# A gated graph network on one core: the order inside the third tick, the place of a relu, and the engine of a subtraction

## The chip, the cores and the metric

The kernel runs on one core of a Trainium2 chip. The metric is the device time of one execution, in microseconds (us). Engines are named as in the profile: PE is TensorE (matrix products; PEld is its loading of weights), DVE is VectorE, ACT is ScalarE, POOL is GpSimd, SP is SyncE, which here only issues transfers (DMAs). Each engine works through its own list of instructions in order, and waits at an instruction until what it needs from others is there.

## The reference, cut to what matters

```python
# x: (64, 256, 256) float32, adj: (64, 256, 256) int32
def gru_cell(inp, h):                      # w_ih, w_hh: (768, 256)
    i_r, i_z, i_n = split(inp @ w_ih.T + b_ih)
    h_r, h_z, h_n = split(h @ w_hh.T + b_hh)
    r = sigmoid(i_r + h_r)
    z = sigmoid(i_z + h_z)
    n = tanh(i_n + r * h_n)
    return (1.0 - z) * n + z * h

h = maximum(layernorm(x), 0.0)             # layer A: gated graph network
for i in range(3):
    m = h @ weight[i]
    aggr = einsum('bst,bsd->btd', adj != 0, m)
    h = gru_cell(aggr, h)
x = x + h
h = maximum(layernorm(x), 0.0)             # layer B: graph attention, 4 heads
v = h @ W.T + b
logits = leaky_relu(l_src + l_dst, 0.2)    # l_src, l_dst: v times a, per head
probs = softmax(where(adj == 1, logits, -9e15))
x = x + einsum('bijh,bjhc->bihc', probs, v)
```

In the last line of the cell, (1 - z) n + z h is n + z (h - n). It is this `h - n` that the change touches.

## The kernel before, in words

**Tiling.** The 64 batch elements are taken in 32 pairs. State, sums and gates lie transposed: 128 partitions, two halves (`c` = 0, 1) of the 256 features, and 2 x 256 nodes of the pair along the free dimension; element `i` = 0 or 1 of the pair is one half of it. A square product of 256 features for one element (`block`, L313) is four fp32 matmuls of 128x128 on 128x256, and each such matmul is two records in the profile, so a block shows as x8.

**Steps and ticks.** One layer of the gated network for one pair is a `Step` of six ticks, `tick_0` to `tick_5` (L459 to L550). A plan (`at`, and `ready`, `step`, `rest` in `plan_pair`) puts every piece of work at a tick number. Pairs start 18 ticks apart (`APART`), and the three steps of a pair start at ticks 0, 12 and 24 of it, so that in any 18 ticks there are three steps one after the other: layer 0 of pair p, layer 2 of pair p - 1, layer 1 of pair p. The profile shows these as steps of 22.4, 25.5 and 28.5 us, and their sum, 76.4 us, as a period. Attention work of earlier pairs is spread over the same ticks.

**What sets the order.** Within a tick the phases are STEP, READY, REST, and in a phase the later pair comes first (L1033: `for tick in sorted(plan)`). The scheduler is off (`manual_schedule`): each engine's list is in the order in which the plan calls the functions. A fractional tick is a tick of its own between two others, so what stands there comes after all of the tick before.

**Products and sums.** The gates of both elements are built from fewer products with sums and differences of weights and states. The names that matter here, with buffer numbers and trailing digits left out in the profile (`p5` shows as `p`, `m5` as `m`, `T1` to `T4` as `T`):

- `state_sums` (L431): T1 = h1 - h0, T3n and T2n, by VectorE, three ticks ahead of their step; `last_state_sum` (L440): T4n.
- `tick_0`: the first part of the state's n gate into bank `qa`, the aggregation `pa` (L470), copied by ScalarE to `aggr` (L474).
- `tick_1`: the part NS2 into `qb` (L482), then VectorE writes the second half of `qb` from its first (L483); block `pc` with `w_h`; ScalarE copies `pc` to `pd` (L489); T3 and T2 by VectorE (L491, L492).
- `tick_2`: parts NS3 and NS4 into the two halves of `qb` (L496, L497; the matmul's own line is L448), VectorE's `hn` from the first half (L498), ScalarE's `hn` from the second (`state_n`, L451), block `p5` from T1, copied by ScalarE to `m5` (L503), T4 by VectorE (L504).
- `tick_3`: block S2 into `pd` from T2, VectorE's `pe` = `pd` + `m5` (L509), block RA into `pc`, tanh of the r gate (L455).
- `tick_4`: a last part into `qb` from T4n, `first_n(0)` (L525), block RZ into `pd` (L518, which writes the bank that L509 reads), Z by VectorE (L519), block S4 into `pe`.
- `tick_5`: `first_n(1)`, the n gate's blocks `pn0` and `pn1`, block ZA into `pd` from T4; `new_n` (L532): tanh by ScalarE (L536), then h - n into `R` by POOL (L540).
- `update(i)` (L552), in the READY phase of the tick after the step: R = (Z + 1) R (L557), h = R / 2 + n (L558), both by VectorE. These are thus in VectorE's list behind `tick_0` and ahead of `tick_1` of the following step.

After `update`, `back` (L788) turns h back by PE (`pback`, L807), ScalarE rounds it to `hNhi` (L797), VectorE writes the remainder `hNlo` (L798); after the last layer VectorE adds the turned h to x instead (L813).

**The relu.** From the third pair on, the normalised rows `xn_a` (L353) are made at tick -10 of their pair; at tick -10 too, in the READY phase, ScalarE takes their relu in place (L771); at tick -9 VectorE splits them in 16 bit words (`halve`, L387), which two DMAs of SP write out (L389) and read back transposed (L393). Tick -10 of a pair falls in the third tick of a layer-2 step. In that tick's READY phase ScalarE also has an attention operation of an earlier pair, `zz<-link` (L921), and in its REST phase the `hNhi` of the second element; the values of the attention, `val` (L868), their `score` (L876) and the transpose of it by PE (`pscore`, L886) belong to the same step.

The banks of PSUM: 5 for the gates (`ps_g`), taken in turn, 3 for the rest (`ps_m`).

Of the kernel before, what the change touches and what calls it, by code (L numbers as in the profile page):

```python
# [14 lines left out]
AF = mybir.ActivationFunctionType  # L15
# [3 lines left out]
P = 128  # L19
# [8 lines left out]
def gated_gnn_then_gat_kernel(  # L28
# [39 lines left out]
    nc = tc.nc  # L68
    B, N, D = x.shape
# [4 lines left out]
    KD = D // P  # L74
# [3 lines left out]
    T = PB * N  # L78
# [121 lines left out]
    w_a = [const.tile([P, KD, 6 * D], F32, name=f"w_a_{l}") for l in range(L)]  # L200
    RH, RZ = range(2)
    N00, N01, N11, NS1, NS2, NS3, NS4 = range(7)
    RA, ZA, NA, S1, S2, S4 = range(6)
# [99 lines left out]
    def flat(y):  # L303
        return y.rearrange("q r d -> q (r d)")
# [4 lines left out]
    def block(pt, w, j, src, start=False):  # L309

        for c in range(KD):
            for k in range(KD):
                nc.tensor.matmul(  # L313
                    pt[:, ts(c, N)], w[:, k, j * D + c * P : j * D + (c + 1) * P], src[:, k, :],
                    start=start and c == 0 and k == 0, stop=(c == KD - 1 and k == KD - 1),
                    skip_group_check=True,
                )
# [9 lines left out]
    def at(tick, phase, p, fn):  # L327
        plan.setdefault(tick, ([], [], []))[phase].append((-p, fn))

    def plan_norm(src, name, p, ticks, relu=False):  # L330


        v = {}

        def stats(r0):
            def fn():
                if not v:
                    v["st"] = small.tile([P, R, 6], F32, tag="st", name=f"st_{name}")
                    v["mv"] = small.tile([P, R, 2], F32, tag="mv", name=f"mv_{name}")
                for r in (r0, r0 + 1):  # L340
                    nc.vector.bn_stats(v["st"][:, r, :], src()[:, r, :])
                    nc.vector.bn_aggr(v["mv"][:, r, :], v["st"][:, r, :])
            return fn

        def deviation():
            rstd = v["rstd"] = small.tile([P, R], F32, tag="rstd", name=f"rstd_{name}")
            nc.vector.tensor_scalar_add(rstd, v["mv"][:, :, 1], EPS)
            nc.gpsimd.tensor_tensor(rstd, rstd, mhalf, ALU.pow)

        def result():  # L350
            xn = v["xn"] = buf("xn", [P, R, D], f"xn_{name}")
            for r in range(R):
                nc.vector.tensor_scalar(  # L353
                    xn[:, r, :], src()[:, r, :], v["mv"][:, r, 0:1], 0.0 if relu else v["rstd"][:, r : r + 1],
                    op0=ALU.subtract, op1=ALU.max if relu else ALU.mult,
                )

        for t, fn in zip(ticks, (stats(0), stats(2), deviation, result)):
            at(t, READY, p, fn)
        return v  # L360

    def plan_relu_T(v, tag, name, p, ticks):

        w = {}

        def fn(k):
            def go():
                if not w:
                    w["hT"] = buf(tag, [P, KD, T], f"hT_{name}")
                pt = bank(f"pt_{name}_{k}")  # L370
                for r in range(R):
                    nc.tensor.transpose(pt[:, ts(r, P)], v["xn"][:, r, ts(k, P)], ident)
                nc.scalar.activation(w["hT"][:, k, :], pt, AF.Relu)
            return go

        for k, t in enumerate(ticks):
            at(t, REST, p, fn(k))
        return w

    def plan_turn(src, tag, name, p, ticks):  # L380


        w = {}

        def halve():
            words = buf("words", [P, R, 2, D], f"words_{name}", U16)
            nc.vector.tensor_copy(words, src().bitcast(U16).rearrange("q r (d w) -> q r w d", w=2))  # L387
            w["rows"] = dram.tile([R, P, 2 * D], U16, tag="words", name=f"words_dram_{name}")
            nc.sync.dma_start(w["rows"].rearrange("r q e -> q r e"), words.rearrange("q r w d -> q r (w d)"))  # L389

        def turn():
            w["turned"] = buf("turned", [P, 2, KD * T], f"turned_{name}", U16)
            nc.sync.dma_start_transpose(  # L393
                w["turned"].rearrange("q w (k n) -> q (w k) n", k=KD), w["rows"].rearrange("r q e -> (r q) e")
            )

        def join():
            w["hT"] = buf(tag, [P, KD, T], f"hT_{name}")
            nc.vector.tensor_copy(
                flat(w["hT"]).bitcast(U16).rearrange("q (n w) -> q n w", w=2), w["turned"].rearrange("q w n -> q n w")  # L400
            )

        at(ticks[0], READY, p, halve)
        at(ticks[1], REST, p, turn)
        at(ticks[2], READY, p, join)
        return w

    def by_c(y):
        return y.rearrange("q (c n) -> q c n", c=KD)

    def of(y, i):
        return y[:, :, ts(i, N)]

    class Step:
# [77 lines left out]
            nc.vector.tensor_add(self.own("T2", [P, KD, N]), T3, h0)  # L492

        def tick_2(self):
            q_b = self.qb
            self.part(q_b[:, :N], NS3, self.T3n)  # L496
            self.part(q_b[:, N:], NS4, of(self.hT(), 1)[:, 1, :])  # L497
            nc.vector.scalar_tensor_tensor(  # L498
                of(self.hn, 1)[:, 1, :], q_b[:, :N], bhn[:, 1:2], self.m5n, op0=ALU.add, op1=ALU.add
            )  # L500
            self.state_n(0, 1, q_b[:, N:])
            block(self.p5, w_a[self.l], S1, self.T1, start=True)
            nc.scalar.copy(self.own("m5", [P, T]), self.p5)  # L503
            nc.vector.tensor_sub(self.own("T4", [P, KD, N]), self.T2, of(self.aggr, 0))  # L504

        def tick_3(self):
            R_ = self.own("R", [P, KD, T])
# [24 lines left out]
        def new_n(self, i):  # L532
            n__ = of(self.hn, i)
            p_n = by_c(getattr(self, f"pn{i}"))
            for c in range(KD):
                nc.scalar.activation(  # L536
                    n__[:, c, :], p_n[:, c, :], AF.Tanh, bias=bi[:, 2 * KD + c : 2 * KD + c + 1]
                )
            if not (self.end and i == 1):
                nc.gpsimd.tensor_sub(of(self.R, i), of(self.hT(), i), n__)  # L540

        def tick_5(self):
# [9 lines left out]
        def update(self, i):  # L552

            d_ = of(self.R, i)
            if self.end and i == 1:
                nc.vector.tensor_sub(d_, of(self.hT(), i), of(self.hn, i))
            nc.vector.scalar_tensor_tensor(d_, of(self.Z, i), 1.0, d_, op0=ALU.add, op1=ALU.mult)  # L557
            nc.vector.scalar_tensor_tensor(of(self.hT(), i), d_, 0.5, of(self.hn, i), op0=ALU.mult, op1=ALU.add)  # L558
# [181 lines left out]
    def plan_pair(p):  # L740
# [5 lines left out]
        def ready(t, fn):  # L746
            at(t0 + t, READY, p, fn)
# [20 lines left out]
        xn_a = plan_norm(lambda: v["x"], f"a{p}", p, [t0 + t for t in norm_ticks])  # L768
        ready(-1 if p else -2.5, to_edge)
        if dma_a:  # L770
            ready(-10, lambda: nc.scalar.activation(flat(xn_a["xn"]), flat(xn_a["xn"]), AF.Relu))  # L771
            h = plan_turn(lambda: xn_a["xn"], "hT_a", f"a{p}", p, [t0 - 9, t0 - 8, t0 - 3])
        else:
            h = plan_relu_T(xn_a, "hT_a", f"a{p}", p, [t0 - 4, t0 - 3])
# [238 lines left out]
    for p in range(NPAIR):  # L1013
        plan_pair(p)
# [52 lines left out]
```

## Time and profile before

| | |
|---|---|
| time, median of 3 executions | 2521.81 us (2521.77 to 2523.39) |
| the profiled execution's own time | 2522.01 us |
| its span, first to last instruction | 2520.2 us |
| PE busy | 2468.9 us, 98% |
| PEld busy | 2189.5 us, 87% |
| DVE busy | 1947.3 us, 77% |
| ACT busy | 1433.9 us, 57% |
| POOL busy | 630.3 us, 25% |
| mean granted TensorE clock | 0.997 of full speed |

Busy time is that of the profiled execution, as a share of its span. A row of a timeline gives the start and the duration in us, the engine, the source line, the operation, the tile written and the tiles read, the shape, and in brackets the idle time of the engine before it and the instruction that ended that idle time. A row of the list of waits gives the waiting instruction, what it waited for, the time in sum, how often, and the longest. Matmuls are pipelined, and the start of one to the start of the next says more than the duration.

### The profile page before, as it was taken

What the parts mean: (1) busy time and instruction counts of PE and PEld (TensorE: products, weight loads), DVE (VectorE), ACT (ScalarE), POOL (GpSimd) and SP (SyncE); (2) the same over time, 40 slices, a digit from 0 to 9 for tenths busy, and PEclk for the clock granted to TensorE, in tenths of its full rate; (3) what the DMA queues carried; (4) which work ended last, traced back from release to release, by engine and by line L of the source; (5) the groups of instructions that cost most, each with busy time, mean ns of one, the idle gap of its engine ahead of it and who ended that gap; (6) DMA issues with size and microseconds to landing.
All of it is one profiled execution on the core that took longest, in us unless ns stands there. A gap on an engine that the chain in (4) does not pass through costs nothing.

```text
span 2520.2 us, 37693 instructions
## 1 busy us (share of the span) xinstructions
PE 2468.9 (98%) x13446; PEld 2189.5 (87%) x13446; DVE 1947.3 (77%) x4576; ACT 1433.9 (57%) x3007; POOL 630.3 (25%) x514
## 2 busy tenths in 40 slices
PE   8999999999999999999999999999999999999998
PEld 6888888888888888888888888888888888888887
DVE  5678877788777788777878777887777887778767
ACT  3445556555555555556555555555565555665664
POOL 0112232222222232222232322222222222222222
PEclk9999999999999999999999999999999999999999
DMA  3025656555656455656556565556565556564455
GB/s 95 17 59 126 152 117 143 128 124 127 155 114 150 119 124 137 135 125 145 116 128 149 122 139 131 121 126 159 109 151 120 126 133 135 126 148 118 107 115 109
DMA packets 322091, 313.73 MB, mean 124 GB/s; under 512 B 166560, under 2 KB 282224, under 8 KB 321904
## 3 DMA queue, kind: packets, MB, share of 16 engines
q1 hardware_dynamic: 286608, 181.29, 27.1%
q0 software_dynamic: 33728, 130.03, 26.9%
q8 instruction: 106, 1.74, 0.3%
q14 instruction: 81, 0.66, 0.1%
q10 hardware_dynamic: 1568, 0.01, 0.0%
HBM read 215.62 MB, written 56.60 MB: 108 GB/s over the span
## 4 chain that ended last, share of the span: by engine, by line
PE 68%; DVE 23%; ACT 6%; issue 2%; DMA 1%; POOL 0%; DVEq 0%; SPq 0%; ACTq 0%; POOLq 0%
PE pd L313 16%; PE pn L313 9%; PE pc L313 9%; PE po L572 7%; PE pe L313 6%; PE qb L448 5%; PE pa L470 5%; PE p L313 4%; PE qa L448 3%; DVE any L948 3%; DVE hT_a L558 2%; DVE val L868 2%; DVE edge L763 2%; DVE hNlo L798 2%; PE pback L807 2%
## 5 line engine op out<-in xcount | busy, mean ns | idle before, releaser
L540 POOL TENSOR_TENSOR R<-hT_a,hn 128x512 f32<-128x512 f32 x191 | 278.2, 1457 | 1250.2 <-ACT hn L536 1175.5
L313 PE MATMUL pn<-aggr,w_a 128*128 128x256 f32 x1536 | 365.1, 380 | 1.8 <-DVE pn L525 1.8
L313 PE MATMUL pd<-T,w_a 128*128 128x256 f32 x1536 | 366.3, 381 | 0.0
L313 PEld LDWEIGHTS pn<-aggr,w_a 128*128 128x128 f32 x1536 | 286.9, 190 | 43.2 <-DVE pn L525 3.2
L313 PEld LDWEIGHTS pd<-T,w_a 128*128 128x128 f32 x1536 | 288.1, 191 | 37.6
L557 DVE SCALAR_TENSOR_TENSOR R<-Z,R 128x512 f32<-128x512 f32 x192 | 134.3, 700 | 215.9 <-POOL R L540 207.5
L572 PEld LDWEIGHTS po<-val,zz 128*128 128x128 f32 x2048 | 244.9, 192 | 4.5
L948 DVE CUSTOM_DVE_ANT_0 any<-drow,noedge 128x256 f32<-128x256 f32 x496 | 238.0, 480 | 9.7 <-DMA drow<-score_dram 1.0
L536 ACT ACTIVATE hn<-pn,bi 128x256 f32<-128x256 f32 x384 | 160.3, 470 | 146.0 <-PE pn L313 145.8
L572 PE MATMUL po<-val,zz 128*128 128x65 f32 x2048 | 242.1, 272 | 0.0
L588 POOL TENSOR_TENSOR x<-x,o 128x256 f32<-128x256 f32 x124 | 136.9, 1105 | 393.3 <-DVE o L583 372.1
L968 ACT ACTIVATE zz<-zz,val 128x256 f32<-128x256 f32 x496 | 224.2, 506 | 0.0
L455 ACT ACTIVATE R<-pc,brz 128x256 f32<-128x256 f32 x192 | 80.5, 470 | 241.6 <-PE pc L313 241.6
L798 DVE TENSOR_TENSOR hNlo<-pback,hNhi 128x512 fp32r<-128x512 f32 x128 | 88.2, 689 | 150.4 <-ACT hNhi L797 150.4
L455 ACT ACTIVATE R<-pe,brz 128x256 f32<-128x256 f32 x192 | 80.5, 470 | 216.2 <-PE pe L313 216.2
L525 DVE SCALAR_TENSOR_TENSOR pn<-R,hn 128x512 f32<-128x512 f32 x192 | 148.6, 774 | 49.3 <-ACT R L455 32.0
L313 PE MATMUL pd<-T,w_h 128*128 128x256 f32 x768 | 183.6, 382 | 0.2 <-DVE pe L509 0.2
L313 PE MATMUL p<-T,w_a 128*128 128x256 f32 x768 | 181.4, 379 | 0.0
L313 PE MATMUL pc<-hT_a,w_h 128*128 128x256 f32 x768 | 181.4, 379 | 0.0
L313 PE MATMUL pc<-aggr,w_a 128*128 128x256 f32 x768 | 181.4, 379 | 0.0
L313 PE MATMUL pe<-aggr,w_a 128*128 128x256 f32 x768 | 181.4, 379 | 0.0
L313 PEld LDWEIGHTS pd<-T,w_h 128*128 128x128 f32 x768 | 143.5, 190 | 24.7 <-DVE pe L509 6.4
(183 smaller groups left out, 5254.8 us busy)
## 6 DMA issues: line engine op xcount, KB each, us to landing
zz<-score_dram POOLq DMA_DIRECT2D x62, 1024.0 KB, 11.8
zz<-topT_dram POOLq DMA_DIRECT2D x62, 1024.0 KB, 8.8
adj<-in_adj_dram SPq DMA_DIRECT2D x64, 512.0 KB
drow<-score_dram SPq DMA_DIRECT2D x62, 512.0 KB
x<-in_x_dram SPq DMA_DIRECT2D x32, 512.0 KB
out_dram<-x SPq DMA_DIRECT2D x31, 512.0 KB
words_dram_a<-words_a SPq DMA_DIRECT2D x30, 512.0 KB
words_dram_b<-words_b SPq DMA_DIRECT2D x29, 512.0 KB
```

Source lines behind the costliest of these rows:

```text
L313: nc.tensor.matmul(pt[:, ts(c, N)], w[:, k, j * D + c * P : j * D + (c + 1) * P], src[:, k, :], start=start and c == 0 and k == 0, stop=(c ...
L448: nc.tensor.matmul(pt, w_n[:, j, :], src, start=start, stop=True, skip_group_check=True)
L455: nc.scalar.activation(of(dst, i)[:, c, :], src[:, c, :], AF.Tanh, bias=brz[:, g0 + c : g0 + c + 1], scale=0.5)
L525: nc.vector.scalar_tensor_tensor(by_c(self.bank(f"pn{i}")), of(self.R, i), 1.0, of(self.hn, i), op0=ALU.add, op1=ALU.mult)
L536: nc.scalar.activation(n__[:, c, :], p_n[:, c, :], AF.Tanh, bias=bi[:, 2 * KD + c : 2 * KD + c + 1])
L540: nc.gpsimd.tensor_sub(of(self.R, i), of(self.hT(), i), n__)
L557: nc.vector.scalar_tensor_tensor(d_, of(self.Z, i), 1.0, d_, op0=ALU.add, op1=ALU.mult)
L572: nc.tensor.matmul(po[:, ts(h_, VC)], zz[:, j, h_, ts(s, P)], v["val"][:, i * KN + j, ts(h_, VC)], start=(j == 0), stop=(j == KN - 1),)
L588: add(v["x"][:, r, :], v["x"][:, r, :], o)
L798: nc.vector.tensor_sub(lo, pt, hi)
L948: nc.vector.tensor_tensor_reduce(any_, drow[r // KN][:, h, :], v["noedge"][:, r, :], 1.0, -3.0e38, ALU.add, ALU.max, accum_out=v["top"][:, ...
L968: nc.scalar.activation(zz[:, h, :], zz[:, h, :], AF.Prelu, alpha=ALPHA, bias=v["val"][:, r, S0 + H + h : S0 + H + h + 1],)
```

## The change

Three edits. In `tick_2` the block `p5` and the copy of it to `m5` come first, ahead of the two `qb` parts, and T4 comes ahead of VectorE's `hn`. The subtraction h - n of the second element leaves `new_n` (POOL) and is made in `update(1)` by VectorE, which before was so only in the very last step. The relu of `xn_a` is put at tick -9.5 instead of -10. What is computed stays the same. No function is new, and nothing else moves.

```diff
         def tick_2(self):
             q_b = self.qb
+            block(self.p5, w_a[self.l], S1, self.T1, start=True)
+            nc.scalar.copy(self.own("m5", [P, T]), self.p5)
             self.part(q_b[:, :N], NS3, self.T3n)
             self.part(q_b[:, N:], NS4, of(self.hT(), 1)[:, 1, :])
+            nc.vector.tensor_sub(self.own("T4", [P, KD, N]), self.T2, of(self.aggr, 0))
             nc.vector.scalar_tensor_tensor(
                 of(self.hn, 1)[:, 1, :], q_b[:, :N], bhn[:, 1:2], self.m5n, op0=ALU.add, op1=ALU.add
             )
             self.state_n(0, 1, q_b[:, N:])
-            block(self.p5, w_a[self.l], S1, self.T1, start=True)
-            nc.scalar.copy(self.own("m5", [P, T]), self.p5)
-            nc.vector.tensor_sub(self.own("T4", [P, KD, N]), self.T2, of(self.aggr, 0))
...
-            if not (self.end and i == 1):
+            if i == 0:
                 nc.gpsimd.tensor_sub(of(self.R, i), of(self.hT(), i), n__)
...
         def update(self, i):
             d_ = of(self.R, i)
-            if self.end and i == 1:
+            if i == 1:
                 nc.vector.tensor_sub(d_, of(self.hT(), i), of(self.hn, i))
...
         if dma_a:
-            ready(-10, lambda: nc.scalar.activation(flat(xn_a["xn"]), flat(xn_a["xn"]), AF.Relu))
+            ready(-9.5, lambda: nc.scalar.activation(flat(xn_a["xn"]), flat(xn_a["xn"]), AF.Relu))
```

## The prediction, made before the changed kernel ran

> **What bounds the kernel.** I read the page first: shares of busy time, then the waits.
>
> ```profile
> PE 2468.9 (98%) x13446; PEld 2189.5 (87%) x13446; DVE 1947.3 (77%) x4576; ACT 1433.9 (57%) x3007; POOL 630.3 (25%) x514
> ...
> PE qb L448 <- DVE qb L483: 16.8, 28, 0.7
> PE pscore L886 <- DVE score L876: 7.1, 29, 0.8
> ...
> PEld pd L313 <- DVE pe L509: 6.4, 29, 0.6
> ...
> DVE R L557 <- POOL R L540: 207.5, 122, 3.3
> ```
>
> TensorE (PE) is the bound: 51.3 us of 2520.2 are not busy, and 24 of them lie in its start and tail (10.8 in the first 78 us, 12.8 in the last 120, by the windows view). So only repeated small holes in the PE can be won. The list of waits names two, `qb` and `pscore`, both about once per pair of batch elements. The 207.5 us that VectorE (DVE) waits for GpSimd (POOL) are no time of the run by themselves.
>
> In the PE's timeline one period (three steps: layer 1, layer 0, layer 2) takes 76.43 us and repeats to within 0.2 us, 27 times, from 269.9 to 2333.7 us. The two holes of one period:
>
> ```profile
> 1220.94 0.60 PE L807 MATMUL pback<-ident,hT_a 128*128 128x128 f32 x4
> 1222.14 0.70 PE L448 MATMUL qb<-T3n,w_n 128*128 128x256 f32 x2 [0.60 <-DVE qb L483]
> 1222.68 0.59 PE L448 MATMUL qb<-hT_a,w_n 128*128 128x256 f32 x2
> 1223.11 1.89 PE L313 MATMUL p<-T,w_a 128*128 128x256 f32 x8
> ...
> 1252.08 1.89 PE L313 MATMUL pc<-aggr,w_a 128*128 128x256 f32 x8
> 1254.19 0.27 PE L886 MATMUL pscore<-ident,score 128*32 128x128 f32 x1 [0.22 <-DVE score L876]
> 1254.30 0.59 PE L448 MATMUL qb<-T4n,w_n 128*128 128x256 f32 x2
> 1254.73 1.96 PE L313 MATMUL pd<-T,w_h 128*128 128x256 f32 x8
> 1256.53 1.89 PE L313 MATMUL pe<-aggr,w_a 128*128 128x256 f32 x8
> ```
>
> Starts tell more than idle time, since ends are modelled. Elsewhere `pback` takes 0.43 from its start to the next start, a pair of `qb` parts 0.43 each, a block 1.73, `pscore` 0.11. Layer-0 step: `p` would start at 1220.94 + 0.43 + 0.86 = 1222.23; it starts at 1223.11, so **0.87 is lost**. Layer-2 step: `pe` would start at 1252.08 + 1.73 + 0.11 + 0.43 + 1.73 = 1256.08; it starts at 1256.53, so **0.45 is lost** (0.38 on `score`, the rest on `pe`, L509, which weights of `pd` wait for). The layer-1 step has no such hole. Total 1.32 per period.
>
> [...] the 0.87 is marked as 0.60 of idle. [...] the `any` below takes 1.49 beside a POOL subtract and 0.42 after it, and ends 0.28 after the subtract does. [...] the trace has 0.68 for `T` (L434), the same shape. [...] here 1457 ns (L540) to 680, 2.1 times.
>
> ```profile
> 1214.91 1.52 POOL L540 TENSOR_TENSOR R<-hT_a,hn 128x512 f32<-128x512 f32 x1 [2.04 <-ACT hn L536]
> ...
> 1215.22 1.49 DVE L948 CUSTOM_DVE_ANT_0 any<-drow,noedge 128x256 f32<-128x256 f32 x1
> 1216.75 0.42 DVE L948 CUSTOM_DVE_ANT_0 any<-drow,noedge 128x256 f32<-128x256 f32 x1
> 1221.66 0.43 DVE L483 TENSOR_TENSOR qb<-qb,m5n 128x256 f32<-128x256 f32 x1
> 1224.74 0.47 DVE L498 SCALAR_TENSOR_TENSOR hn<-qb,bhn,m5n 128x256 f32<-128x256 f32 x1
> 1227.50 0.69 DVE L798 TENSOR_TENSOR hNlo<-pback,hNhi 128x512 fp32r<-128x512 f32 x1 [0.55 <-ACT hNhi L797]
> 1228.11 0.69 DVE L509 TENSOR_TENSOR pe<-pd,m 128x512 f32<-128x512 f32 x1
> ```
>
> **Part 1, the h - n of the second element.** It takes 95 subtracts from POOL and gives VectorE 95 of 0.68, 65 us of busy time. In the layer-1 and layer-2 steps VectorE was waiting there anyway: in layer 2 the tanh ends at 1238.95, POOL's subtract at 1240.52, L557 starts at 1240.56; VectorE itself, free at 1239.37, would be done at about 1239.97: 0.55 earlier (layer 1 alike, 0.6). In the layer-0 step VectorE runs without a pause from 1209.04 to 1228.2, so the subtract is paid: 0.72 from start to start. But the `any` no longer blocks: -1.07 (1.49 - 0.42). The sum there is **-0.35**: L483 starts at 1221.31 instead of 1221.66. What else POOL has, adds of `x` (L588) and DMA issues, moves earlier, with no one waiting for it; the L588 that lengthens an L558 to 1.10 moves with its `o` and still does.
>
> **Part 2, block first.** PE order in the third tick is now `p` (1.73), two `qb` parts (0.86), `pback`. `p` needs T1 (three ticks old) and runs from 1221.37 to 1223.10; L483 ends at 1221.74, so `qb` does not wait: +0.87 back, covered by 1.36 us of margin. ScalarE (ACT) copies `m` before the state activation, which queues behind L498 (it waits for VectorE, not PE). VectorE does T4 (0.60) before L498; L498 then waits for the parts: in layer 1 until about 1195.7 instead of 1193.95, absorbed by 1.21 idle ahead of L509 at 1199.70.
>
> **What is late next.** In the layer-0 step PE now wants weights for `pd` (L518's block) at 1228.95 - 0.87 = 1228.08, and these must wait for L509 to have read `pd`. L509 stands behind `hNlo`, which waits for `hNhi` (L797) on ACT, behind the state activation, behind L498. After: L498 at 1224.74 - 0.35 + 0.60 = 1224.99, ends 1225.46; activation 1225.49 (before 1225.24); it no longer has the 0.46 of the `m` copy behind it, so `hNhi` at 1225.49 + 0.38 + 0.81 = 1226.68 (before 1226.89); `hNlo` 1227.29, L509 1227.90 to 1228.59. Weights at 1228.65; in the layer-2 hole weights that waited so started at 1254.70 and the next block's 1.62 later, not 1.72. So 0.57 - 0.10 = **0.47 is lost again** and 0.87 - 0.47 = 0.40 stays.
>
> **Part 3, relu half a tick later.** ACT in the layer-2 step:
>
> ```profile
> 1249.83 1.06 ACT L771 ACTIVATE xn_a<-xn_a 128x1024 f32<-128x1024 f32 x1 [0.94 <-DVE xn_a L353]
> 1250.79 1.04 ACT L921 ACTIVATE zz<-link 128x1024 f32<-128x1024 bf16 x1
> 1251.74 0.56 ACT L797 CAST hNhi<-pback 128x512 fp32r<-128x512 f32 x1
> ```
>
> Relu now follows L921 and `hNhi`. With L498 at 1248.3 (parts end at 1248.27), activation 1248.8, L921 1249.2, `hNhi` 1250.2, relu 1250.7 to 1251.8. `hNlo` at 1250.8 (before 1252.34), `val` x2, `score` done at 1252.5, L509 done at 1253.1. PE wants `pscore` weights at 1253.6 and `pd` weights at 1254.1: both holes close, **+0.45**. `words` (L387) needs relu and comes after L509: 1253.0 instead of 1254.56, so its two SP DMAs start earlier, not later. L921 moves up 1.6 us; its `link` transfer was issued 30 us before. If `link` landed late, `hNhi` would be late as before and at most this 0.45 is lost.
>
> **Sum.** 28 x (0.40 + 0.45) = 23.8 us (28 occurrences by the wait list). The profiled execution took 2522.01: 2498.2. The median of the runs is 0.20 below it: **2498.0**.
>
> **Unknowns.** The added subtract: below, 0.60 (its pipelined cost, `T` to T3n); above, 1.1, if a POOL add blocks it as it does L558. The block on `any` is gone or not: 0 or 1.07. The end of L509 follows both one to one, until its 1228.02, from where nothing is lost.
>
> **Rivals.** (a) VectorE has more room than I reckon and L509 is in time: 28 x 1.32 = 37 us, 2485. For: 0.57 is a difference of long chains. Against: no link of the chain has slack. Chance 0.12. (b) L509 later by another 0.4, all of the 0.87 lost again: 28 x 0.45 = 12.6, 2509. For: ACT's leaky pair (L968) and POOL's add stand there. Chance 0.16. (c) Slower: the `any` is not freed (something else on POOL moves into its place), VectorE in the layer-0 step is 0.72 later instead of 0.35 earlier, L509 ends at 1229.66, 1.07 later than forecast: lost 0.47 + 1.07 = 1.54, net -0.67 + 0.45 = -0.22, 28 times: 2528; a blocked subtract (1.1) makes it 2539. It turns the sign once L509 ends after 1229.44. Against: POOL has nothing else queued there. Chance 0.08 slower; 0.06 for halfway, within 0.2% (5 us, about what a measurement here can tell from no change). The forecast: 0.58, own range 2493 to 2504. That p doesn't come first isn't a rival: the instruction order of the built kernel shows it.
>
> Range: (a) and most of (b), 2486 to 2511. Faster 0.58 + 0.12 + 0.16 = 0.86.
>
> **What would show it.** Right: no `qb` wait for L483 and no `pscore` wait on PE; a wait of `pd` weights for `pe` (its L509), some 28 of 0.5; period 75.6; layer-0 step 22.0, layer-2 step 25.1, layer-1 unchanged at 28.5; `any` near 0.42 throughout; VectorE 1947 + 65 - 30 (28 x 1.07) = 1982 busy. Wrong: a layer-0 step longer than 22.4, or a new wait in the layer-1 step, where `pn` (L525, done 1211.75, weights 1211.85) has 0.1 of margin.

## The result, and the profile after

The changed kernel takes 2498.32 us (median of 5, 2496.31 to 2499.02) beside 2521.80 us of the kernel before on the same chip: ratio 0.990, 95% interval 0.9887 to 0.9914. The forecast was 2498.0. Lines of the changed kernel are one higher than before from the third tick on, so L509 is now L510, L540 is L541; L498 has become L502, and L557 is now the added subtract.

The page's busy times, and then rows of the list of waits (who waits, for whom, us in sum, times, longest):

```profile
PE 2464.2 (99%) x13446; PEld 2191.9 (88%) x13446; DVE 1992.2 (80%) x4671; ACT 1437.5 (58%) x3007; POOL 494.3 (20%) x419
```

```profile
DVE R L558 <- POOL R L541: 126.3, 58, 3.4
...
DVE hn L502 <- PE qb L448: 52.9, 67, 2.6
...
PEld pd L313 <- DVE pe L510: 14.5, 29, 0.8
```

PE has the same instructions in a shorter run. The wait of `qb` for L483 (28 times before) is in no row, `pscore` waits once in place of 29 times, and the weights of `pd` now wait 29 times for L510, 0.5 each. VectorE has 95 instructions and 45 us more.

The PE's timeline, layer-0 step and then layer-2 step of one period:

```profile
1212.19 1.89 PE L313 MATMUL p<-T,w_a 128*128 128x256 f32 x8
1213.92 0.59 PE L448 MATMUL qb<-T3n,w_n 128*128 128x256 f32 x2
...
1218.68 0.59 PE L448 MATMUL qb<-T4n,w_n 128*128 128x256 f32 x2
1219.38 1.99 PE L313 MATMUL pd<-T,w_h 128*128 128x256 f32 x8
1221.21 1.89 PE L313 MATMUL pe<-aggr,w_a 128*128 128x256 f32 x8
...
1242.41 1.89 PE L313 MATMUL pc<-aggr,w_a 128*128 128x256 f32 x8
1244.13 0.27 PE L887 MATMUL pscore<-ident,score 128*32 128x128 f32 x1
...
1246.40 1.89 PE L313 MATMUL pe<-aggr,w_a 128*128 128x256 f32 x8
```

From `p` to `qb` it is 1.73, the block's own time: the first hole is closed. From the last `qb` pair to `pe` it would be 0.43 + 1.73 = 2.16; it is 2.53: **0.37 of the 0.87 has come back one block later**, ahead of `pd`. In the layer-2 step `pscore` follows `pc` by 1.72, and `pe` comes 3.99 behind `pc`, where 1.73 + 0.11 + 0.43 + 1.73 = 4.00 is the undisturbed spacing: that hole is closed and nothing follows.

Steps are measured from the `qa<-hT_a` that opens one to the next; these two open the layer-0 and the layer-2 step, 21.89 apart:

```profile
1206.34 0.65 PE L448 MATMUL qa<-hT_a,w_n 128*128 128x256 f32 x2
...
1228.23 0.59 PE L448 MATMUL qa<-hT_a,w_n 128*128 128x256 f32 x2
```

| median step, us | layer 2 | layer 1 | layer 0 | time, us |
|---|---|---|---|---|
| before | 25.53 | 28.52 | 22.38 | 2521.80 |
| changed | 25.07 | 28.52 | 21.89 | 2498.32 |

### The profile page after: what moved, and what is told of

The parts are those of the page before. It is cut to its first block, busy times and chain, and to the rows that moved or that the text cites. A ratio compares the mean times of both kernels' runs of the same rounds, so it can differ in the third digit from the quotient of the medians.

```text
span 2496.3 us, 37566 instructions
## 1 busy us (share of the span) xinstructions
PE 2464.2 (99%) x13446; PEld 2191.9 (88%) x13446; DVE 1992.2 (80%) x4671; ACT 1437.5 (58%) x3007; POOL 494.3 (20%) x419
## 4 chain that ended last, share of the span: by engine, by line
PE 83%; DVE 12%; ACT 3%; issue 1%; DMA 1%; POOL 0%; SPq 0%; ACTq 0%; DVEq 0%; POOLq 0%
PE pd L313 18%; PE pn L313 13%; PE pc L313 9%; PE po L573 8%; PE pe L313 7%; PE pa L470 5%; PE qb L448 5%; PE p L313 5%; PE pv L864 5%; PE qa L448 4%; PE pback L808 2%; DVE hT_a L559 2%; DVE any L949 2%; DVE R L558 2%; DVE hNlo L799 1%
## 5 line engine op out<-in xcount | busy, mean ns | idle before, releaser
L541 POOL TENSOR_TENSOR R<-hT_a,hn 128x512 f32<-128x512 f32 x96 | 141.9, 1479 | 1124.5 <-ACT hn L537 1042.5
L949 DVE CUSTOM_DVE_ANT_0 any<-drow,noedge 128x256 f32<-128x256 f32 x496 | 209.1, 422 | 9.3 <-DMA drow<-score_dram 0.5
L526 DVE SCALAR_TENSOR_TENSOR pn<-R,hn 128x512 f32<-128x512 f32 x192 | 149.1, 777 | 77.3 <-ACT R L455 54.7
L313 PEld LDWEIGHTS pd<-T,w_h 128*128 128x128 f32 x768 | 143.5, 190 | 32.8 <-DVE pe L510 14.5
```

Source lines behind the costliest of these rows:

```text
L313: nc.tensor.matmul(pt[:, ts(c, N)], w[:, k, j * D + c * P : j * D + (c + 1) * P], src[:, k, :], start=start and c == 0 and k == 0, stop=(c ...
L526: nc.vector.scalar_tensor_tensor(by_c(self.bank(f"pn{i}")), of(self.R, i), 1.0, of(self.hn, i), op0=ALU.add, op1=ALU.mult)
L949: nc.vector.tensor_tensor_reduce(any_, drow[r // KN][:, h, :], v["noedge"][:, r, :], 1.0, -3.0e38, ALU.add, ALU.max, accum_out=v["top"][:, ...
```

## The experiments

All were built from the changed kernel by undoing or moving parts. The times of the kernel before beside them were 2522.1 to 2522.3 us. Each table row gives medians of the steady part (24 periods) as above, the time as the median of its runs, and the ratio to the kernel before with its 95% interval.

| kernel | layer 2 | layer 1 | layer 0 | time, us | ratio |
|---|---|---|---|---|---|
| block first alone | 25.82 | 28.52 | 22.30 | 2533.39 | 1.0045 (1.0033 to 1.0057) |
| subtract alone | 25.53 | 28.52 | 21.97 | 2509.04 | 0.9947 (0.9935 to 0.9959) |
| relu alone | 25.07 | 28.52 | 22.38 | 2512.22 | 0.9956 (0.9943 to 0.9969) |
| block and subtract | 25.81 | 28.52 | 21.89 | 2520.34 | 0.9990 (0.9982 to 0.9998) |
| block and relu | 25.07 | 28.52 | 22.30 | 2509.19 | 0.9943 (0.9929 to 0.9958) |
| subtract and relu | 25.07 | 28.52 | 21.97 | 2495.99 | 0.9888 (0.9873 to 0.9903) |
| changed, T4 last | 25.07 | 28.52 | 21.51 | 2488.14 | 0.9859 (0.9840 to 0.9878) |
| changed, subtract on both | 25.07 | 28.52 | 22.96 | 2527.70 | 1.0021 (1.0014 to 1.0028) |
| changed, subtract moved in layer 1 only | 25.07 | 28.52 | 21.89 | 2497.76 | 0.9897 (0.9884 to 0.9911) |
| T4 last, block first in layer 0 only | 25.07 | 28.52 | 21.52 | 2483.52 | 0.9850 (0.9833 to 0.9866) |

The theory: the parts work on one chain. L509 is the next thing late, and T4 delays it while the freed `any` (the attention's maximum on VectorE, L948 before and L949 after) brings it forward. The rival: the parts add up, and block first closes the layer-0 hole.

### One part alone

Block first alone (against the changed kernel):

```diff
-            if i == 0:
+            if not (self.end and i == 1):
                 nc.gpsimd.tensor_sub(of(self.R, i), of(self.hT(), i), n__)
...
-            if i == 1:
+            if self.end and i == 1:
                 nc.vector.tensor_sub(d_, of(self.hT(), i), of(self.hn, i))
...
-            ready(-9.5, lambda: nc.scalar.activation(...Relu))
+            ready(-10, lambda: nc.scalar.activation(...Relu))
```

> Only the third tick is changed; the subtract of the second element stays on POOL and the relu stays at tick -10. Theory of the prediction (one chain, in which L509 is late next): in the layer-0 step the subtract beside the `any` still holds VectorE up, L498 now stands behind T4, so L509 ends some 0.4 us later than in the changed kernel and nearly all of the 0.87 is lost again (0.79); in the layer-2 step L498 waits for the later `qb` parts, relu and `hNhi` follow it, and the 0.45 hole grows to about 0.8. Sum: 28 x (-0.08 + 0.34) = +7, 2529 us, slower than before. Rival (the parts add up, and block first alone brings the 0.49 of the layer-0 step): 2521.8 - 28 x 0.49 = 2508 us.

It is slower, by 11 us. The steps are 22.30 and 25.82, where the theory had 22.30 and 25.87; they account for 28 x 0.21 = 5.9 us, and the rest lies mostly in the first pairs. The rival falls: block first by itself brings 0.08 in the layer-0 step and costs 0.29 in the layer-2 step.

Subtract alone (the third tick in its old order, the relu back at -10):

```diff
             q_b = self.qb
-            block(self.p5, w_a[self.l], S1, self.T1, start=True)
-            nc.scalar.copy(self.own("m5", [P, T]), self.p5)
             self.part(q_b[:, :N], NS3, self.T3n)
...
-            nc.vector.tensor_sub(self.own("T4", [P, KD, N]), self.T2, of(self.aggr, 0))
...
             self.state_n(0, 1, q_b[:, N:])
+            block(self.p5, w_a[self.l], S1, self.T1, start=True)
+            nc.scalar.copy(self.own("m5", [P, T]), self.p5)
+            nc.vector.tensor_sub(self.own("T4", [P, KD, N]), self.T2, of(self.aggr, 0))
...
-            ready(-9.5, lambda: nc.scalar.activation(...Relu))
+            ready(-10, lambda: nc.scalar.activation(...Relu))
```

> Only the subtract of the second element goes to VectorE. Theory: the `any` of the layer-0 step is no longer held up (1.49 to 0.42), L483 comes 0.41 us earlier, and the hole ahead of `qb` shrinks from 0.87 to 0.46, while L509 moves with it: 28 x 0.41 = 11.5, 2510 us. Rival (the subtract is neutral or costs, since VectorE gets 65 us more work): 2522 us or more.

2509.04, layer-0 step 21.97: VectorE got 65 us more work and the kernel became 13 us faster.

Relu alone (both other parts undone as in the two diffs above, the relu left at -9.5):

> Only the relu is put at tick -9.5. Theory and rival agree here: the 0.45 of the layer-2 step is gone, and nothing else: 28 x 0.45 = 12.6, 2509 us, layer-2 step 25.1, layer-0 step 22.4.

The steps are as expected. Of its six runs three took 2508.7 to 2508.9 us, as expected, and three 2515.5 to 2515.8, so the median 2512.22 is the time of neither, and the ratio in the table stands between them too. The profiled execution is one of the longer ones: its last 370.6 us have a granted TensorE clock of 0.97, where the same last steps of the kernel before take 365.1 at 0.99. That is no part of the relu's own effect in the steps.

### One part undone

Relu back (only the last pair of lines of the first diff):

> The changed kernel with the relu back at tick -10. Theory: layer-0 step as in the changed kernel (21.9), layer-2 step worse than before (25.5 + 0.34 = 25.9), since L498 waits for the later parts, and relu, L921 and `hNhi` stand behind the activation that follows it: 2498.3 + 28 x 0.79 = 2520 us. Rival (the parts add up): 2498.3 + 12.6 = 2511 us.

2520.34, layer-2 step 25.81: without the relu's half tick, the change would have been worth 0.1%.

Subtract back on POOL (only the first two pairs of lines of the first diff):

> The changed kernel with the subtract of the second element back on POOL. Theory: without the freed `any`, VectorE in the layer-0 step is 0.4 us later, L509 ends 0.4 us later and the step is 22.3 instead of 21.9; layer-2 step 25.1: 2498.3 + 28 x 0.41 = 2510 us. Rival (the subtract is neutral, VectorE's added work is merely hidden): 2498 us.

2509.19, layer-0 step 22.30: the subtract is worth 0.41 there, as when it stands alone.

Old order of the third tick (the second diff without its relu lines):

> The changed kernel with the third tick in its old order. Theory: the subtract alone already takes 0.41 of the 0.87 hole, and the chain behind L509 holds the block-first order to little more, so layer-0 step 21.97 instead of 21.89, layer-2 step 25.1: 2498.3 + 28 x 0.08 = 2500.5 us, less a part of the 1 to 2 us that the block-first order loses in the first pairs. Rival (block first is what closes the hole): layer-0 step 22.4, 2512 us.

2495.99, 2.3 us below the changed kernel. The steps are as expected, the time is not: the theory had 2498.5 to 2500.5. In the company of the other two, block first as the change has it gains 0.08 per period (28 x 0.08 = 2.2) and loses more than that in the first pairs.

### The two suspects inside the parts

T4 behind VectorE's `hn` again, the block still first:

```diff
             self.part(q_b[:, N:], NS4, of(self.hT(), 1)[:, 1, :])
-            nc.vector.tensor_sub(self.own("T4", [P, KD, N]), self.T2, of(self.aggr, 0))
             nc.vector.scalar_tensor_tensor(
...
             self.state_n(0, 1, q_b[:, N:])
+            nc.vector.tensor_sub(self.own("T4", [P, KD, N]), self.T2, of(self.aggr, 0))
```

> The changed kernel with T4 behind VectorE's `hn` again, the block still first. Theory: T4 (0.59 from start to start) is what makes the state activation, `hNhi`, `hNlo` and so L509 late; L509 ends 0.54 earlier, before PE wants the weights, the rest of the hole (0.38) closes: layer-0 step 21.5, 2498.3 - 28 x 0.38 = 2487.5 us; at most 0.1 per layer-1 step back, where `pn` has little margin. Rival (L509 is held by something else, such as the copy to `m5` or PE itself): 2498 us, with the wait of `pd` weights for `pe` still 0.5, 28 times.

2488.14, layer-0 step 21.51. In VectorE's timeline of that kernel `hn` (L501 here) follows `hNlo` at once, and L510 ends at 1215.24; PEld's row shows weights of `pd` with no wait ahead of them:

```profile
1211.06 0.68 DVE L799 TENSOR_TENSOR hNlo<-pback,hNhi 128x512 fp32r<-128x512 f32 x1
1211.66 0.47 DVE L501 SCALAR_TENSOR_TENSOR hn<-qb,bhn,m5n 128x256 f32<-128x256 f32 x1
...
1214.55 0.69 DVE L510 TENSOR_TENSOR pe<-pd,m 128x512 f32<-128x512 f32 x1
```

```profile
1215.41 1.70 PEld L313 LDWEIGHTS pd<-T,w_h 128*128 128x128 f32 x8
```

POOL makes the subtract too, and VectorE makes it over that:

```diff
-            if i == 0:
+            if not (self.end and i == 1):
                 nc.gpsimd.tensor_sub(of(self.R, i), of(self.hT(), i), n__)
```

> The changed kernel, but POOL makes the subtract of the second element as before, too, and VectorE makes it once more over that (the same numbers are written twice). Theory: this puts the block on the `any` back with VectorE's subtract still there, 1.07 us in the layer-0 step: L509 ends 1.07 later and the step is 22.9 to 23.0; 2498.3 + 28 x 1.07 = 2528 us, slower than the kernel before. Rival (the `any` was long for another reason than POOL's subtract, or there is room for it): 2498 to 2505 us.

2527.70, layer-0 step 22.96. POOL's and VectorE's timelines of that kernel, and its list of waits on PE: the `any` is long again, though VectorE does the same work as in the changed kernel. Its subtract must now also wait for POOL's, but in the steady layer-0 steps that wait is 0; in the other two steps it is 1.2 to 1.3 us, and these steps take 25.07 and 28.52 as in the changed kernel.

```profile
1219.59 1.50 POOL L541 TENSOR_TENSOR R<-hT_a,hn 128x512 f32<-128x512 f32 x1 [2.05 <-ACT hn L537]
```

```profile
1219.89 1.48 DVE L949 CUSTOM_DVE_ANT_0 any<-drow,noedge 128x256 f32<-128x256 f32 x1
```

```profile
PE pd L313 <- DVE pe L510: 32.8, 28, 1.3
```

This is also the prediction's slower rival, brought about: it was worked out as 2528 for an `any` that stays blocked.

The subtract on VectorE in layer-1 steps only:

```diff
-            if i == 0:
+            if i == 0 or not (self.end or self.l == 1):
                 nc.gpsimd.tensor_sub(of(self.R, i), of(self.hT(), i), n__)
...
-            if i == 1:
+            if i == 1 and (self.end or self.l == 1):
                 nc.vector.tensor_sub(d_, of(self.hT(), i), of(self.hn, i))
```

> The changed kernel, but VectorE makes the second element's subtract only in the layer-1 steps, whose update falls into the layer-0 step; in the layer-0 and layer-2 steps it is on POOL as before. Theory: the whole worth of moving the subtract is the `any` freed in the layer-0 step, so this runs like the changed kernel: layer-0 step 21.9, layer-2 step 25.1, 2498 us, with VectorE about 43 us less busy than there. Rival (the shorter chain tanh, subtract, update of the other two steps counts too): 2503 us or more.

2497.76, the steps of the changed kernel, VectorE 1946.5 us busy in place of 1992.2. A third of the moved subtracts does all the good.

### A version that beats both

T4 last, and the block first only in layer-0 steps from the third pair on:

```diff
         def tick_2(self):
             q_b = self.qb
+            first = self.l == 0 and int(self.n_.split("_")[0]) >= 2
+            def sums():
+                block(self.p5, w_a[self.l], S1, self.T1, start=True)
+                nc.scalar.copy(self.own("m5", [P, T]), self.p5)
+            if first:
+                sums()
...
             self.state_n(0, 1, q_b[:, N:])
+            if not first:
+                sums()
+            nc.vector.tensor_sub(self.own("T4", [P, KD, N]), self.T2, of(self.aggr, 0))
```

> The previous experiment with T4 last, but the block comes first only in the layer-0 steps from the third pair on; every other step has the old order of the third tick. Theory: in the steady part this is as with T4 last (21.5, 25.1, 28.5), since only the layer-0 step has a hole that the order closes, and the first pairs no longer lose the 3 to 4 us that the block-first order costs them: 2488.1 - 3.5 = 2484.5 us. Rival (the order is needed in the other steps too, where nothing shows it, or the early loss has another cause): 2488 us or more.

2483.52 (2483.23 to 2490.77), 38 us below the kernel before and 15 below the changed one. Three early steps are back where they were before: the 1st, 3rd and 8th step take 39.14, 27.30 and 23.72 us, in the changed kernel 40.21, 29.21 and 24.80.

## Why the prediction was right, step by step

**Part 1, the subtract.** Right in sign and size. In VectorE's timeline of the changed kernel (9.18 us earlier in the run than before, counted at the `rden` that waits for PE in both):

```profile
1206.03 0.41 DVE L949 CUSTOM_DVE_ANT_0 any<-drow,noedge 128x256 f32<-128x256 f32 x1
...
1212.07 0.43 DVE L483 TENSOR_TENSOR qb<-qb,m5n 128x256 f32<-128x256 f32 x1
...
1215.15 0.68 DVE L501 TENSOR_TENSOR T<-T,aggr 128x512 f32<-128x512 f32 x1
1215.74 0.48 DVE L502 SCALAR_TENSOR_TENSOR hn<-qb,bhn,m5n 128x256 f32<-128x256 f32 x1
...
1218.03 0.69 DVE L799 TENSOR_TENSOR hNlo<-pback,hNhi 128x512 fp32r<-128x512 f32 x1 [0.54 <-ACT hNhi L798]
1218.64 0.69 DVE L510 TENSOR_TENSOR pe<-pd,m 128x512 f32<-128x512 f32 x1
```

The `any` takes 0.41, and L483 starts at 1212.07 + 9.18 = 1221.25 (forecast 1221.31, before 1221.66). That POOL's subtract is what blocked the `any` is shown both ways: 1.49 beside it, 0.41 without it, 1.48 where POOL makes it again. Of all 512 `any` of a run, 28 take over 1 us in the kernel before and one in the changed kernel (1.49 in the tail, beside POOL's 1.59 for the subtract of a first element). In the kernel where both engines subtract, `pd` on PE waits 28 times for L510, 32.8 us in all. Why the subtract holds the `any` up, these runs don't tell.

**Part 2 and what is late next.** Right in mechanism, with the loss priced 0.10 too high. L510 ends at 1219.33 + 9.18 = 1228.51 (forecast 1228.59) and 0.37 to 0.38 is lost again (forecast 0.47). T4, which the prediction priced at 0.60 ahead of L498, is shown to be the cause by the experiment with T4 last.

**Part 3, the relu.** Right: 25.53 - 25.07 = 0.46 (forecast 0.45). ScalarE's timeline has the order L922, `hNhi`, relu, with `hNhi` ahead:

```profile
1239.53 1.05 ACT L922 ACTIVATE zz<-link 128x1024 f32<-128x1024 bf16 x1
1240.47 0.57 ACT L798 CAST hNhi<-pback 128x512 fp32r<-128x512 f32 x1
1240.94 1.07 ACT L772 ACTIVATE xn_a<-xn_a 128x1024 f32<-128x1024 f32 x1
```

The forecast chain holds link by link: brought to the time scale of before (+9.67, counted at the `hNlo` that opens it), L502 starts at 1248.30 (forecast 1248.3), `hNhi` at 1250.14 (1250.2), and L510 ends at 1253.06 (1253.1). The prediction priced the relu with block first in place and didn't ask what it is worth without. With the old relu, block first makes the layer-2 hole 0.29 larger, since VectorE's `hn` waits for the later `qb` parts and relu and `hNhi` stand behind it. The half tick pays 0.74 in this company (25.81 to 25.07), 0.46 alone.

**Layer-1 step.** Right: 28.52 as before. The wait of L502 for PE (1.30 us in the layer-1 step) is there and absorbed.

**The sum.** Two errors cancelled. The period became 0.95 shorter (forecast 0.85): 28 x 0.95 = 26.6 in place of 23.8, by the 0.10 of part 2. The first pairs lost 4.1 us in the three steps named above (1.07 + 1.91 + 1.08 by the step times of the changed kernel less those of the last experiment), which the prediction didn't count at all: it covered L498's later wait in the steady layer-1 step and left the first pairs out. That leaves 22.5; most of the other 1.0 of the measured 23.5 came from the 4th step (21.78 to 21.35) and the last 71 us of the run (0.76 shorter). So the agreement of 2498.32 with 2498.0 is in part luck. In the 8th step L502's wait (1.30 us) is not absorbed, as VectorE has no idle time from there to L526; `pn` of the PE, before and then in the changed kernel:

```profile
214.87 2.00 PE L313 MATMUL pn<-aggr,w_a 128*128 128x256 f32 x8 [0.21 <-DVE pn L525]
...
220.13 1.99 PE L313 MATMUL pn<-aggr,w_a 128*128 128x256 f32 x8 [1.55 <-DVE pn L525]
```

```profile
218.31 1.97 PE L313 MATMUL pn<-aggr,w_a 128*128 128x256 f32 x8 [1.33 <-DVE pn L526]
...
223.48 1.99 PE L313 MATMUL pn<-aggr,w_a 128*128 128x256 f32 x8 [1.49 <-DVE pn L526]
```

**VectorE's busy time** came out at 1992.2 (forecast 1982): the subtracts added 65.8 and the `any` gave back 28.9, both as priced; the other 8 us is spread and was not traced.

## What to carry to other kernels

A hole closed on the engine that bounds is worth only what the next late arrival leaves of it (here 0.49 of 0.87), so follow the chain to the next consumer before pricing the gain; here the order of two VectorE instructions decided 10 us, and one edit that alone cost 11 us came out near neutral in company. Edits on one chain don't add: run them apart and together. Where a steady loop gains by an order, look at the first rounds too, and give the order only to the steps that need it.

## What the runs showed that was not expected

Moving work to the busier engine made it no later: a VectorE subtract of 0.68 cost less than the 1.07 for which POOL's had blocked an unrelated VectorE operation.

A hole early in the run was followed by a slow clock, and in the changed kernel that cost more than the hole (by estimate 3.4 us, half of a slow stretch of 6.83, beside 2.3). In the 3rd step PE waits for three small weight products, 2.3 us in all with block first and 1.9 with the old order, and 1.28 at the longest. About the last of them the granted clock falls to half of full speed. In the changed kernel it stays there for 6.83 us (that step takes 29.21 us), and its mean from 90 to 115 us is 0.86, as it is in "block first alone". With the old order in that step it is 3.41 us in the kernel before (27.30), with a mean of 0.93, as in "subtract alone"; "subtract and relu" and "T4 last, block first in layer 0 only" have means of 0.85 and 0.84 from 90 to 101 us (joined from two windows), which is 3.4 us at half speed too.

So of the 1.91 by which the changed kernel's 3rd step is longer, 0.39 goes with the longer hole (1.28 in place of 0.89 at the first product), and the other 1.5 with a slow stretch twice as long: 3.41 us at half speed cost 1.7, by estimate. By the step times the order need not bring that: with block first in every step, the step takes only 27.69 in "block and subtract" and 27.68 in "subtract moved in layer 1 only"; with the old order it takes 25.62 in "relu alone", 1.68 less than in the kernel before. What decides how long the clock stays low is not shown.
